# Layer 1's graph attention: projection of raw rows on centred weights, scores spread by DMA, and another order of mask loads

## The chip, the cores and the metric

The kernel runs on one core of a Trainium2 chip. The metric is the device time of one execution in microseconds (us). A core has five engines that run beside each other and meet in semaphores: TensorE (PE in the profile; PEld is its weight load), VectorE (DVE), ScalarE (ACT), GpSimd (POOL) and SyncE (SP, which here only issues DMAs). ACT, POOL and SP have each a queue for DMAs of their own; all of them share 16 DMA engines.

## What is computed

A network of two layers on 2708 rows of 256 numbers, each with a graph attention and a feed-forward part with experts. The change is in layer 1's graph attention:

```python
def _L1_gnn_ref(X, adj, W, b, S):        # X is the layernorm of x
    Xp = X @ W.T + b
    f = Xp.shape[1]
    n = X.shape[0]
    a_src = Xp @ S[:f]
    a_dst = Xp @ S[f:]
    e = jax.nn.leaky_relu(a_src[:, None] + a_dst[None, :])   # slope 0.01
    mask = (adj != 0) | jnp.eye(n, dtype=bool)
    e = jnp.where(mask, e, -jnp.inf)
    attn = jax.nn.softmax(e, axis=1)
    return jax.nn.sigmoid(attn @ Xp)
...
x = x + _L1_gnn_ref(_layernorm(x, axis=-1), adj, L1_gnn_W, L1_gnn_b, L1_gnn_S)
x = x + _L1_ffn_ref((_layernorm(x, axis=-1))[None], ...)[0]
```

With s = a_src of row i and d = a_dst of neighbour j, a weight before the division by its row's sum is exp(max(s + d, 0.01 (s + d))). A factor that depends on i alone falls out in that division, so exp(s) may be taken out, and what is left is max(exp(d), exp(0.01 d - 0.99 s)).

## The kernel before

Rows go in 22 tiles of 128 (P; the last has 20), columns in two halves (KC = 2). Stages follow one another: `first` (layer 0's attention parts), `experts_blocks` for layer 0, `second` (layer 1's graph attention and its routing), `experts_blocks` for layer 1. The change is in `second` (line 1416) and in the weight preparation of `first` (`weight_folds`, line 311).

**The order** inside `first` and `second` is not written by hand. Each step is given to a `Plan` (line 74) by `add(engine, length, run, needs, take, give, rank, lands)`: an estimated length, the steps it needs, the buffers it takes and gives back, a rank, and for a DMA the time to land. `issue` simulates the engines with these estimates, at each moment lets the engine with the lowest ranked startable step go on, and emits instructions in that order. Every engine then runs its own list strictly in order. Where the plan sees TensorE idle for over 1.0 us, it puts in matmuls of no use (`nobody`, line 1670), which cover 0.75 of the gap.

**`experts_blocks` for layer 0** leaves two blocks of expert 7 (`LATE`) for `second`, whose weights lie in the upper half of `arena`. Each expert block ends in a scatter that adds its rows in DRAM (`add_rows`, line 617, on GpSimd's queue).

**`second`.** `some_blocks` (line 524) does the two LATE blocks: rows fetched (534), transposed (539), three `up` steps (561), gate, two `down` steps (584), and the join by line 617. Beside them, five DMAs on SP bring X from DRAM (1519, 1527); those for tiles 10 and up wait for LATE's joins. `prepare(t)` makes a tile's features:

- `stats` (VectorE, 267, 269, 1458) and `power` (GpSimd, 1462) give mean and inverse deviation, `scale` (1466) the normalised rows xn,
- `turn` (1472) transposes xn on TensorE, `back` (ACT, 1476) copies it out of PSUM,
- `times`: line 1481 multiplies by the 258 columns of `wx[1]` (256 of W, then W times both halves of S, so that columns 256 and 257 are s and d); line 1484 multiplies `wsb`, which is column 256 repeated 128 times, by the tile, so that s of its 128 rows stands on every partition,
- `parts` (VectorE, 1488, 1489) keeps s and d in `sd`, and `dcol`, which is -0.99 d plus a constant `shift`; `features` (ACT) copies s into `sb` (1492), writes exp(d) into the last column of `hb` (1493) and the features times exp(d) into the others (1494).

PSUM's banks limit this: `mm` has two, and each is held from `times` to the end of `features`.

`aggregate` then goes through four groups of six tiles i (the last has four). For each of the 22 tiles j: `weigh` (ACT, 1560) makes E = exp(-0.99 s + dcol) for the group's 768 rows, `mask` (VectorE) turns the loaded masks to 0 and 1 (1569), sets the diagonal (1573) and makes PT = max(E, 1) times mask (1575), and TensorE adds PT times `hb` to the group's accumulators, six products of two records each (1582). E and PT have three buffers each. After a group, `mean`, a sigmoid, `join` and the routing follow beside the next group's products.

The masks lie in DRAM as rows (`mb`) and are turned by DMA transposes on SP, one for each tile i. Group 0's go to `arena` in two halves (1549): the first to its lower half, after the first three X loads; the second to its upper half, where LATE's weights lie, after LATE's joins. Those of groups 1 to 3 (1545) are issued six at a time into one of two places, when it is free.

**`weight_folds`** works out the extra columns early in `first`: it writes them to `wx[1]` (339) and spreads column 256 into `wsb` (341). `centre` (866) is there already for layer 0's weights: it sums the rows of a weight by a matmul with ones (872) and takes the column means off (876).

Of the kernel before, what the change touches and what calls it, by code (L numbers as in the profile page):

```python
# [20 lines left out]
P = 128  # L21
N = 2708
C = 256
# [126 lines left out]
def adj_ffn_kernel(ctx, tc, x, adj, vecs, bias_rows, tab, w_gnn0, w_gnn1, wqkv, wo,  # L150
# [155 lines left out]

    wsb = const.tile([P, KC, P], F32, name="wsb")
    shift = const.tile([P, 1], F32, name="shift")
    wnorm = const.tile([P, 1], F32, name="wnorm")

    def weight_folds(add, pool, tile_, needs, rank):

        fold = small.tile([P, 2, KC], F32, name="fold", bufs=1)
        for w, col in ((wg[0], V_C1), (wg[1], V_SS)):
            v = {}

            def turn(w=w, v=v):
                v["pt"] = tile_().rearrange("p (k i c) -> p k i c", k=KC, i=KC)
                for k in range(KC):
                    for i in range(KC):  # L320
                        nc.tensor.transpose(v["pt"][:, k, i, :], w[:, i, k * P:(k + 1) * P], ident)

            def back(v=v):
                v["wT"] = pool.tile([P, KC, C], F32, tag="rT", name="wT", bufs=1)
                nc.scalar.copy(v["wT"].rearrange("p k c -> p (k c)"), v["pt"].rearrange("p k i c -> p (k i c)"))

            def times(v=v, col=col):
                v["pc"] = tile_()[:, :2 * KC].rearrange("p (i a) -> p i a", i=KC)
                for i in range(KC):
                    for k in range(KC):  # L330
                        nc.tensor.matmul(v["pc"][:, i, :], v["wT"][:, k, i * P:(i + 1) * P],
                                         vec[:, col + k:col + k + KC + 1:KC], start=(k == 0), stop=(k == KC - 1))

            def norm(v=v):
                wc = small.tile([P, KC, 2], F32, name="wc", bufs=1)
                nc.scalar.activation(wc, v["pc"], AF.Square, accum_out=wnorm)

            def spread(v=v):
                nc.vector.tensor_copy(wx[1][:, :, C:], v["pc"])
                for k in range(KC):  # L340
                    nc.vector.tensor_copy(wsb[:, k, :], wx[1][:, k, C:C + 1].to_broadcast([P, P]))

            a = add("PE", 0.6, turn, needs, take=["mm"], rank=rank)
            a = add("ACT", 0.6, back, [a], take=["rT"], give=["mm"], rank=rank)
            a = add("PE", 1.0, times, [a], take=["mm"], give=["rT"], rank=rank)
            if col == V_C1:
                add("ACT", 0.4, norm, [a], give=["mm"], rank=rank)
            else:
                add("DVE", 0.7, spread, [a], give=["mm"], rank=rank)
        v = {}  # L350
# [14 lines left out]
        a = add("PE", 0.3, sum_up, [a], take=["mm"], rank=rank)  # L365
        add("DVE", 0.2, shifted, [a], give=["mm"], rank=rank)


# [419 lines left out]
    def first(X, XB, norms, tops, hd, mb, xs, acc, arena, load_weights):  # L788
# [11 lines left out]
        with ExitStack() as s:  # L800
# [431 lines left out]
            folded = add("DVE", 0.4, fold, [rest], rank=1.0)  # L1232
            weight_folds(add, af, mm_tile, [rest], 45.0)
            cleared = [add("SP", 2.5, lambda e=e: clear(xs[0], e), [loaded[10 + e]], rank=10.5 + e, lands=3.0)
# [181 lines left out]
    def second(X, XB, xs0, x1, x2, sd, mb, xs, arena, load_weights):  # L1416
# [5 lines left out]


        groups = [range(i, min(i + GI, NT)) for i in range(0, NT, GI)]
        F = C + 1
        with ExitStack() as s:
# [6 lines left out]
            sb = keep.tile([P, N], F32, name="sb")  # L1433
            dcol = keep.tile([P, NT], F32, name="dcol")


# [8 lines left out]
            add = plan.add  # L1445
            made, normed, got = [], [], []

            def prepare(t):
# [3 lines left out]

                bank = "po" if t < 8 else "mm"
                xt = X[:r, t, :]

                def stats():
                    v["mv"], v["pv"] = moments(xt, r), small.tile([P, 1], F32, tag="pv", name="pv")
                    nc.vector.tensor_scalar(v["pv"][:r], v["mv"][:r, 1:2], 1.0, 1e-5, ALU.mult, ALU.add)

                def power():  # L1460
                    v["rs"] = small.tile([P, 1], F32, tag="prs", name="prs")
                    nc.gpsimd.tensor_tensor(out=v["rs"][:r], in0=v["pv"][:r], in1=mhalf[:r, 0:1], op=ALU.pow)

                def scale():
                    v["xn"] = work.tile([P, C], F32, tag="xn", name="xn")
                    nc.vector.tensor_scalar(v["xn"][:r], xt, v["mv"][:r, 0:1], v["rs"][:r],
                                            ALU.subtract, ALU.mult)

                def turn():
                    v["pt"] = pt = (pso if bank == "po" else psm).tile([P, 4, P], F32, tag=bank, name="pt")  # L1470
                    for k in range(KC):
                        nc.tensor.transpose(pt[:, k, :r], v["xn"][:r, k * P:(k + 1) * P], ident[:r, :r])

# [4 lines left out]
                def times():  # L1478
                    v["pn"] = pn = psm.tile([P, 4 * P], F32, tag="mm", name="pn")
                    for k in range(KC):  # L1480
                        nc.tensor.matmul(pn[:r, :C + 2], v["xT"][:, k, :r], wx[1][:, k, :],
                                         start=(k == 0), stop=(k == KC - 1))
                    for k in range(KC):
                        nc.tensor.matmul(pn[:, 3 * P:3 * P + r], wsb[:, k, :], v["xT"][:, k, :r],
                                         start=(k == 0), stop=(k == KC - 1))

                def parts():
                    nc.vector.tensor_copy(sd[:r, t, :], v["pn"][:r, C:C + 2])
                    nc.vector.tensor_scalar(dcol[:r, t:t + 1], sd[:r, t, 1:2], SLOPE - 1.0, shift[:r], ALU.mult, ALU.add)

                def features():
                    nc.scalar.copy(sb[:, t * P:t * P + r], v["pn"][:, 3 * P:3 * P + r])
                    nc.scalar.activation(hb[:r, t, C:], v["pn"][:r, C + 1:C + 2], AF.Exp)
                    nc.scalar.activation(hb[:r, t, :C], v["pn"][:r, :C], AF.Copy, scale=hb[:r, t, C:])

                a = add("DVE", 0.85, stats, [loads[sum(t >= e for e in ends)]], take=["mv"], rank=rank)
                a = add("POOL", 0.6, power, [a], rank=rank)
                a = add("DVE", 0.42, scale, [a], take=["xn"], give=["mv"], rank=rank)
                a = add("PE", 0.3, turn, [a], take=[bank], give=["xn"], rank=rank)
                a = add("ACT", 0.4, back, [a], take=["xT"], give=[bank], rank=rank)  # L1500
                a = add("PE", 1.3, times, [a], take=["mm"], give=["xT"], rank=rank)
                b = add("DVE", 0.3, parts, [a], rank=rank)
                made.append(add("ACT", 0.9, features, [a, b], give=["mm"], rank=rank))

# [11 lines left out]

            loads, late, ends = [], [], (2, 7, LATE_T, NT - 1)
            for a, b in zip((0,) + ends, ends):
                loads.append(add("SP", 0.45 * (b - a), lambda a=a, b=b: nc.sync.dma_start(
                    out=X[:, a:b, :], in_=x1[a * P:b * P, :].rearrange("(t p) c -> p t c", p=P)),  # L1520
                    late, rank=-9.0, lands=12.5 if a == 0 else 11.0 if a < LATE_T else 7.0))
                if b == LATE_T:
# [7 lines left out]
            numbered = add("POOL", 0.3, lambda: nc.gpsimd.iota(  # L1530
                XR[:, :, C:C + 1].bitcast(I32), pattern=[[P, NT], [0, 1]], base=0, channel_multiplier=1), late, rank=-5.0)
            for t in range(NT):
                prepare(t)

            def aggregate(g, tiles):
# [4 lines left out]

                def masks():
                    v["mk"] = mks[int(side[g][-1])]
                    for i in tiles:
                        a = (i - tiles[0]) * P
                        nc.sync.dma_start_transpose(out=v["mk"][:, :, a:a + P], in_=mb[i * P:(i + 1) * P, :])

                def masks_by_tile(half):
                    for i in range(half * GI // 2, (half + 1) * GI // 2):
                        nc.sync.dma_start_transpose(out=by_tile[:, i, :, :], in_=mb[i * P:(i + 1) * P, :])

                if g == 0:
                    a = add("SP", 2.8 * GI // 2, lambda: masks_by_tile(0), loads[:3], take=[side[g]], rank=-8.0, lands=2.0)
                    got.append(add("SP", 2.8 * GI // 2, lambda: masks_by_tile(1), [a] + late, rank=-8.0, lands=2.0))
                else:
                    got.append(add("SP", 2.8 * len(tiles), masks, got[-1:], take=[side[g]], rank=rank, lands=2.0))

# [5 lines left out]
                def mask(j):  # L1562
# [11 lines left out]
                    v["PT", j] = p = work.tile([P, GI * P], F32, tag="PT", name="PT")  # L1574
                    nc.vector.scalar_tensor_tensor(wide(p), wide(v["E", j]), 1.0, m, ALU.max, ALU.mult)  # L1575

# [9 lines left out]
                for j in range(NT):  # L1586
                    a = add("ACT", 0.85, lambda j=j: weigh(j), [made[j]] + [made[i] for i in tiles], take=["E"],
                            rank=rank + j)
# [804 lines left out]
```

## Time and profile before

| | |
|---|---|
| median of 3 runs | 1506.64 us (1506.54 to 1509.68) |
| the profiled execution | 1506.29 us, of which its span 1504.5 |
| mean granted TensorE clock | 0.982 |
| TensorE busy in the span | 1417.7 us, 94% |
| VectorE, ACT, GpSimd busy | 762.5, 567.4, 529.9 us |
| line 1582, the products | 968 records, 228.5 us, first at 870.8, last at 1127.5 |
| line 1481, the 258 columns | 88 records, from 839.7 to 906.8 |
| line 1484, the scores on every partition | 88 records, from 840.7 to 907.4 |
| line 1560, the exponentials | 88, first at 855.0 |

A line of a group of instructions names the line of the kernel, the engine, the operation, what it writes and reads, and the shapes; then come the busy time, the mean of one in ns, and how long the engine stood idle just before them, with what ended the wait. In a line of the timeline the first two numbers are start and length in us. A line of busy time by stretch gives the engines' busy us in that stretch, then the granted clock (1.00 is full), the busy share of the DMA engines and what they moved.

### The profile page before, as it was taken

The page shows a single profiled execution, that of the slowest core. Times are in us where ns is not written, and L with a number is a line of the kernel's source. Part 1 is how long each engine was busy: PE and PEld are TensorE (multiplying, and loading weights), DVE is VectorE, ACT ScalarE, POOL GpSimd, SP SyncE. Part 2 cuts the span into 40 slices and gives each one's busy share as a digit, 9 for nine tenths or more (in the row PEclk, how much of TensorE's full clock was granted, in tenths as well). Part 3 has the DMA queues.
Part 4 walks back from the last instruction along what each step waited for, and adds up shares of the span by engine and source line. Part 5 has one row for each costly group of instructions (what it writes and reads, how often), then busy time and mean ns, then how long its engine had stood idle before and what let it go on. Part 6 is the DMA issues. An engine that isn't in the chain of part 4 may idle for free. (4 is left out here: it accounts for less than half of the span.)

```text
span 1504.5 us, 21112 instructions
## 1 busy us (share of the span) xinstructions
PE 1417.7 (94%) x7488; PEld 1030.2 (68%) x7488; DVE 762.5 (51%) x1647; ACT 567.4 (38%) x1134; POOL 529.9 (35%) x681
## 2 busy tenths in 40 slices
PE   5878989989999999999999989999999999999995
PEld 5633433433335888888888778888769878888884
DVE  5688999966676322222222564766745322222221
ACT  2576776755554322222221443444323212122220
POOL 5577668782152221222222310030434122222222
PEclk9999999999999999999999999999999999999998
DMA  7599757430011666656411860633412965566111
GB/s 261 190 298 291 256 193 235 146 121 8 7 41 42 172 194 176 182 150 185 113 15 22 183 133 1 137 80 98 154 48 75 273 190 140 160 173 169 15 18 20
DMA packets 198519, 201.83 MB, mean 134 GB/s; under 512 B 93248, under 2 KB 168520, under 8 KB 195696
## 3 DMA queue, kind: packets, MB, share of 16 engines
q1 hardware_dynamic: 173782, 170.96, 37.4%
q0 software_dynamic: 20352, 25.85, 9.7%
q10 hardware_dynamic: 4270, 3.58, 0.7%
q8 instruction: 61, 1.00, 0.3%
q14 instruction: 54, 0.44, 0.1%
HBM read 128.46 MB, written 56.37 MB: 123 GB/s over the span
## 5 line engine op out<-in xcount | busy, mean ns | idle before, releaser
L2065 PE MATMUL pup<-xTs,arena 128*128 128x256 f32 (+2 forms) x1320 | 252.8, 350 | 0.6 <-ACT xTs L2048 0.6
L2065 PEld LDWEIGHTS pup<-xTs,arena 128*128 128x128 f32 (+1 forms) x1320 | 219.5, 190 | 28.3 <-PE y L2130 2.3
L1582 PE MATMUL po<-hb,PT 128*128 128x257 f32 (+2 forms) x968 | 228.5, 390 | 4.0 <-DVE PT L1575 4.0
L2069 ACT ACTIVATE sl<-pup 128x256 f32<-128x256 f32 (+1 forms) x210 | 73.6, 350 | 370.8 <-PE pup L2065 369.1
L1582 PEld LDWEIGHTS po<-hb,PT 128*128 128x128 f32 (+2 forms) x968 | 177.3, 189 | 44.0 <-issue 13.1
L2070 DVE TENSOR_TENSOR hT<-sl,pup 128x256 f32<-128x256 f32 (+1 forms) x210 | 79.6, 379 | 229.0 <-ACT sl L2069 228.7
L1106 ACT ACTIVATE e<-stt 128x1024 f32<-128x1024 f32 (+1 forms) x132 | 125.4, 986 | 93.6 <-PE stt L1100 68.5
L617 POOL DMA_INDIRECT out<-ys,XR x45 | 69.4, 1542 | 246.7 <-DVE ys L2083 110.0
L1145 DVE TENSOR_TENSOR es<-es,e 128x1024 f32<-128x1024 f32 x104 | 138.0, 1327 | 29.8 <-ACT e L1106 23.1
L617 POOL DMA_INDIRECT acc<-ys,XR x45 | 69.8, 1552 | 226.3 <-DVE ys L2083 94.5
L1100 PE MATMUL stt<-qT,kT 64*128 64x512 f32 (+1 forms) x528 | 132.6, 612 | 6.3 <-ACT e L1106 6.1
L2080 PE MATMUL y<-arena,hT 128*128 128x256 f32 x612 | 136.7, 379 | 0.0
L1809 POOL DMA_INDIRECT xs<-XR,place x88 | 93.4, 1061 | 92.8 <-DVE mk L1569 41.3
L2080 PEld LDWEIGHTS y<-arena,hT 128*128 128x128 f32 x612 | 114.3, 190 | 14.5
L1126 PE MATMUL o<-e,V 128*64 128x512 f32 (+1 forms) x528 | 123.3, 590 | 0.0
L1560 ACT ACTIVATE E<-sb,dcol 128x768 f32<-128x768 f32 (+1 forms) x88 | 75.1, 859 | 108.5 <-DVE PT L1575 108.2
L2083 DVE TENSOR_SCALAR ys<-y,XR 128x256 f32<-128x256 f32 x71 | 34.3, 484 | 141.2 <-PE y L2080 141.1
L2065 PE MATMUL pup<-xTs,room 128*128 128x256 f32 (+3 forms) x528 | 99.9, 346 | 0.0
L1100 PEld LDWEIGHTS stt<-qT,kT 64*128 64x128 f32 x528 | 44.4, 187 | 78.1 <-issue 61.7
L2065 PEld LDWEIGHTS pup<-xTs,room 128*128 128x128 f32 (+1 forms) x528 | 85.4, 189 | 9.8 <-PE y L2130 0.8
L1126 PEld LDWEIGHTS o<-e,V 128*64 128x64 f32 x528 | 33.2, 137 | 69.9 <-issue 55.4
L974 DVE MAX8 tops<-arena 128x8 f32<-128x2708 f32 (+1 forms) x22 | 65.3, 2970 | 1.8 <-DMA arena<-in_adj 1.8
(316 smaller groups left out, 2026.0 us busy)
## 6 DMA issues: line engine op xcount, KB each, us to landing
more<-in_w SPq DMA_DIRECT2D x60, 640.0 KB
arena<-in_adj SPq DMA_DIRECT2D x21, 1354.0 KB
arena<-in_w SPq DMA_DIRECT2D x36, 640.0 KB
mb<-mb SPq DMA_DIRECT2D x44, 352.0 KB
XR<-xs SPq DMA_DIRECT2D x80, 134.0 KB
xs<-none SPq DMA_DIRECT2D x16, 536.0 KB
room<-in_w SPq DMA_DIRECT2D x12, 640.0 KB
acc<-X SPq DMA_DIRECT2D x21, 128.0 KB
```

The costliest lines, as they stand in the source:

```text
L617: nc.gpsimd.indirect_dma_start(out=acc[:, :], out_offset=bass.IndirectOffsetOnAxis(ap=tokens.bitcast(I32), axis=0), in_=ys, in_offset=None ...
L1100: nc.tensor.matmul(st[:r, g, c0(sb):], kT[a:b, sb * P:sb * P + r], qT[a:b, t0 + (sb == t0 + 1):t0 + 2, :, :], start=True, stop=True)
L1106: nc.scalar.activation(e[:r, :, c0(sb):], v[sb, "st"][:r, :, c0(sb):], AF.Exp, scale=1.0 / HD ** 0.5)
L1126: nc.tensor.matmul(v["o"][g * HD:(g + 1) * HD, c:], V[:r, sb, g * HD:(g + 1) * HD], v[sb][:r, g, c:], start=(n + i == 0), stop=(n + i == t ...
L1145: nc.vector.tensor_tensor(es, es, v[sb][:r, :, c:], ALU.add)
L1560: nc.scalar.activation(e[:q, :n], sb[:q, i0:i1], AF.Exp, bias=dcol[:q, j:j + 1], scale=SLOPE - 1.0)
L1582: nc.tensor.matmul(v["po", i][:r, :F], v["PT", j][:q, a:a + r], hb[:q, j, :], start=(j == 0), stop=(j == NT - 1))
L1809: i = nc.gpsimd.indirect_dma_start(out=xs[:, :], out_offset=bass.IndirectOffsetOnAxis(ap=at, axis=0), in_=src, in_offset=None)
L2065: nc.tensor.matmul(pp[:to, i, :B, :], wn[:, c, :], xT[:, c, :B, :], start=(c == 0), stop=(c == KC - 1))
L2069: nc.scalar.activation(sl[:, :B, :], pp[:, 0, :B, :], AF.Silu)
L2070: nc.vector.tensor_tensor(hT[:, n, :B, :], sl[:, :B, :], pp[:, 1, :B, :], ALU.mult)
L2080: nc.tensor.matmul(y, hT[:, n, b, :], w[3][:, n, :], start=(n == 0), stop=(n == NHC - 1))
```

## The change

- **Projection.** `centre` is called for `wx[1]` with its two extra columns, after `weight_folds`. `prepare` transposes the raw rows of X; the product is multiplied by the inverse deviation `rsx` when it is copied out. `stats` and `power` become steps of their own for pairs of tiles (`factors`), and are needed by `parts` only; `power` has two GpSimd instructions. The `scale` step, `wsb` and line 1484 are gone.
- **Scores.** `parts` writes s and d as before, scaled by `rsx`. When a group's tiles have theirs, ACT's queue stores the group's s to a row in DRAM, and then loads that row into `sb` on all 128 partitions. `weigh` needs that load.
- **Limit.** `hb` keeps the features without exp(d) and a column of ones; exp(d) goes into `ecol`, and line 1575 takes max(E, exp(d)). `dcol` has 0.01 d.
- **Masks and loads.** The first half of group 0's masks is issued ahead of the X loads, with no step to wait for but the use of its place; the second half waits for LATE's last `down`. Masks of the other groups are a step for each tile. X's loads are cut at other tiles, and the plan's estimates of loads and masks are other ones.

```diff
-                for k in range(KC):
-                    nc.vector.tensor_copy(wsb[:, k, :], wx[1][:, k, C:C + 1].to_broadcast([P, P]))
...
-            weight_folds(add, af, mm_tile, [rest], 45.0)
+            centre(wx[1], wx[1], C + 2, [weight_folds(add, af, mm_tile, [rest], 45.0)], 45.0)
...
+            ecol = keep.tile([P, NT], F32, name="ecol")
+            rsx = keep.tile([P, NT], F32, name="rsx1")
+            nc.gpsimd.memset(hb[:, :, C:], 1.0)
...
+            srow = dram.tile([1, NT * P], F32, name="srow")
+
+            def factors(tiles):
...
+                def power():
+                    r, k, t = rows(tiles[0]), len(tiles), tiles[0]
+                    pv = small.tile([P, 2], F32, tag="pv2", name="pv2")
+                    nc.gpsimd.tensor_scalar(pv[:r, :k], v["mv"][:r, :k, 1], 1.0, 1e-5, ALU.mult, ALU.add)
+                    nc.gpsimd.tensor_tensor(out=rsx[:r, t:t + k], in0=pv[:r, :k], in1=mhalf[:r, :k], op=ALU.pow)
...
-                bank = "po" if t < 8 else "mm"
+                bank = "po" if t < LATE_T else "mm"
...
-                        nc.tensor.transpose(pt[:, k, :r], v["xn"][:r, k * P:(k + 1) * P], ident[:r, :r])
+                        nc.tensor.transpose(pt[:, k, :r], xt[:, k * P:(k + 1) * P], ident[:r, :r])
...
-                    for k in range(KC):
-                        nc.tensor.matmul(pn[:, 3 * P:3 * P + r], wsb[:, k, :], v["xT"][:, k, :r],
-                                         start=(k == 0), stop=(k == KC - 1))
 
                 def parts():
-                    nc.vector.tensor_copy(sd[:r, t, :], v["pn"][:r, C:C + 2])
-                    nc.vector.tensor_scalar(dcol[:r, t:t + 1], sd[:r, t, 1:2], SLOPE - 1.0, shift[:r], ALU.mult, ALU.add)
+                    nc.vector.tensor_scalar(sd[:r, t, :], v["pn"][:r, C:C + 2], rsx[:r, t:t + 1], None, ALU.mult)
+                    nc.vector.tensor_scalar(dcol[:r, t:t + 1], sd[:r, t, 1:2], SLOPE, shift[:r], ALU.mult, ALU.add)
 
                 def features():
-                    nc.scalar.copy(sb[:, t * P:t * P + r], v["pn"][:, 3 * P:3 * P + r])
-                    nc.scalar.activation(hb[:r, t, C:], v["pn"][:r, C + 1:C + 2], AF.Exp)
-                    nc.scalar.activation(hb[:r, t, :C], v["pn"][:r, :C], AF.Copy, scale=hb[:r, t, C:])
+                    nc.scalar.activation(hb[:r, t, :C], v["pn"][:r, :C], AF.Copy, scale=rsx[:r, t:t + 1])
+
+                def factor():
+                    nc.scalar.activation(ecol[:r, t:t + 1], sd[:r, t, 1:2], AF.Exp)
...
+                b = add("DVE", 0.45, parts, [a, c], rank=rank)
+                parted.append(b)
+                a = add("ACT", 0.5, features, [b], give=["mm"], rank=rank)
+                made.append(add("ACT", 0.2, factor, [a], rank=rank))
...
-            loads, late, ends = [], [], (2, 7, LATE_T, NT - 1)
+            loads, late, ends = [], [], (2, 6, LATE_T, 16, NT - 1)
...
-                    late, rank=-9.0, lands=12.5 if a == 0 else 11.0 if a < LATE_T else 7.0))
+                    late, rank=-9.0, lands=4.0))
...
-                    a = add("SP", 2.8 * GI // 2, lambda: masks_by_tile(0), loads[:3], take=[side[g]], rank=-8.0, lands=2.0)
-                    got.append(add("SP", 2.8 * GI // 2, lambda: masks_by_tile(1), [a] + late, rank=-8.0, lands=2.0))
+                    half = GI // 2
+                    a = add("SP", 3.2 * half, lambda: masks_by_tile(0, half), [], take=[side[g]], rank=-10.0, lands=2.0)
+                    through = [e["needs"][0]["needs"][0] for e in late]
+                    got.append(add("SP", 3.2 * half, lambda: masks_by_tile(half, GI), [a] + through, rank=-9.5, lands=2.0))
                 else:
-                    got.append(add("SP", 2.8 * len(tiles), masks, got[-1:], take=[side[g]], rank=rank, lands=2.0))
+                    a = got[-1]
+                    for i in tiles:
+                        a = add("SP", 3.2, lambda i=i: masks(i), [a], take=[side[g]] * (i == tiles[0]), rank=rank, lands=2.0)
+                    got.append(a)
+
+                def spread_out():
+                    nc.scalar.dma_start(out=srow[0, i0:tiles[-1] * P + P].rearrange("(t p) -> p t", p=P),
+                                      in_=sd[:, tiles[0]:tiles[-1] + 1, 0])
+
+                def spread_in():
+                    nc.scalar.dma_start(out=sb[:, i0:i1], in_=srow[:, i0:i1].to_broadcast([P, n]))
+
+                a = add("ACT", 0.5, spread_out, [parted[i] for i in tiles], rank=-7.0 + g, lands=3.0)
+                row_in = add("ACT", 0.5, spread_in, [a], rank=-7.0 + g, lands=3.0)
...
-                    nc.vector.scalar_tensor_tensor(wide(p), wide(v["E", j]), 1.0, m, ALU.max, ALU.mult)
+                    nc.vector.scalar_tensor_tensor(wide(p), wide(v["E", j]), ecol[:q, j:j + 1], m, ALU.max, ALU.mult)
...
-                    a = add("ACT", 0.85, lambda j=j: weigh(j), [made[j]] + [made[i] for i in tiles], take=["E"],
+                    a = add("ACT", 0.85, lambda j=j: weigh(j), [made[j], row_in], take=["E"],
```

## Prediction

> **What bounds the kernel now.** I read the page's costliest groups first, then the busy time by stretch, then the order of time around the one stretch where TensorE is not full. Layer 1's products, line 1582, are its second largest group:
>
> ```profile
> L1582 PE MATMUL po<-hb,PT 128*128 128x257 f32 (+2 forms) x968 | 228.5, 390 | 4.0 <-DVE PT L1575 4.0
> ```
>
> They run from 870.8 to 1127.7 us, and TensorE idles only 4.0 us before them, once. The stretches before and after the first product (busy us of TensorE, its weight loads, VectorE, ScalarE, GpSimd; granted clock; DMA share; GB/s):
>
> ```profile
> 853.00:860.00 7.00, 5.22 (x29) 4.02 (x27) 2.24 (x11) 6.08 (x18) 0.54 (x1) 1.00 1.13 251
> ...
> 865.00:870.00 5.00, 1.58 (x8) 1.28 (x8) 0.83 (x3) 0.18 (x1) 0.21 (x1) 0.93 1.07 229
> 870.00:876.00 6.00, 5.23 (x12) 4.20 (x13) 5.55 (x17) 2.57 (x5) 1.08 (x2) 0.50 1.05 228
> ...
> 890.00:940.00 50.00, 50.00 (x252) 44.08 (x251) 23.59 (x51) 22.18 (x48) 0.06 (x1) 1.00 0.00 1
> ```
>
> From 890 on TensorE is full and nothing else is; before, there is a hole at 867 to 870.8 and then a clock of 0.50 until 876. So in this stage two things are worth time: the moment of the first product, and every matmul taken away behind it. What ends the hole, on TensorE and VectorE, and what SP issues, in order of time (start, length):
>
> ```profile
> 866.22 0.60 PE L1484 MATMUL pn<-xTs,wsb 128*128 128x128 f32 x4
> ...
> 869.03 0.36 DVE L1569 TENSOR_SCALAR arena<-arena 128x768 bf16<-128x768 bf16 x1 [4.22 <-DMA arena<-mb]
> ...
> 869.76 0.96 DVE L1575 SCALAR_TENSOR_TENSOR PT<-E,arena 128x768 f32<-128x768 f32 x1
> ...
> 870.77 5.94 PE L1582 MATMUL po<-hb,PT 128*128 128x257 f32 x14 [3.95 <-DVE PT L1575]
> ```
>
> ```profile
> 830.48 1.86 SPq L1519 DMA_DIRECT2D X<-acc  x3
> 832.38 12.32 SPq L1549 DMA_TRANSPOSE arena<-mb  x3
> 851.29 0.38 SPq L1519 DMA_DIRECT2D X<-acc  x1
> 851.77 0.52 SPq L1527 DMA_DIRECT2D X<-acc  x1
> 852.39 13.81 SPq L1549 DMA_TRANSPOSE arena<-mb  x3
> 866.25 19.45 SPq L1545 DMA_TRANSPOSE mk<-mb  x6
> ```
>
> VectorE waits 4.22 us for the second half of group 0's masks, issued 852.39 to 866.2 and landed at 868.9, after the last LATE join (line 617, 847.45) and two X loads. The first exponential ran at 855.0, so its own inputs were ready 14 us earlier. **The masks, not the preparation, set the first product.**
>
> **What the Trainium skill says.** (1) "DMA: Bandwidth & Descriptors", section "Rules for kernel authors": a run that is not contiguous is lowered to one descriptor per element, and a DMA that reads what another wrote must wait for its completion. The trace of before has no 4-byte store, so neither is shown. (2) The same page, "Queues, rings and completion order": a DMA engine takes turns between queues packet by packet. The trace agrees in kind: line 617's scatters land in 3.7 to 5.8 us, the longest being the one issued beside the mask transposes. (3) "TensorE: Matmul & The Clock Gate", part 1: an idle window of about 3.4 us halves the clock. Agrees: 3.95 us idle, then 0.50.
>
> **The change, part by part.** The sum is made against the profiled execution, 1506.29 us (span 1504.5); the median of the runs is 0.35 higher.
>
> *Matmuls removed.* Per tile, line 1484's four records go. Their worth is the spacing in the full stretch:
>
> ```profile
> 882.21 1.04 PE L1481 MATMUL pn<-wg,xTs 128*128 128x258 f32 x4
> 883.09 0.61 PE L1484 MATMUL pn<-xTs,wsb 128*128 128x128 f32 x4
> 883.53 1.90 PE L1582 MATMUL po<-hb,PT 128*128 128x257 f32 x8
> ```
>
> 0.88 us for line 1481, 0.44 for 1484, and 0.22 for the two transposes (881.12 to 881.34). A tile's preparation on TensorE falls from 1.54 to 1.10 us.
>
> *First half of the masks moved* ahead of the X loads on SP. It needs only the arena's lower half, which expert 6's last line-2080 matmuls leave at 809.2, so it runs about 809 to 819 (three at 3.3 us, as line 1545 shows) and lands by 822. It meets line 617's scatters at 817.5: up to 2.1 us (5.8 less 3.7) on one of them, so X loads start at 830.5 to 832.6. The plan puts tile 0's transpose into the gap at 838.6, after LATE's second `up`; X landed 2.8 us after issue before, so this is covered, by 3 us. *Second half*: released by LATE's last `down` (846.6 before; I take 845, as the gap is filled sooner) instead of the join; 3 x 3.3 us, then 2.2 to land: 857. Behind it on SP wait the three X loads for tiles 10 to 21, from 851.3 to about 855; they land about 862 and are used behind the first product. The group-1 masks follow, as before, to some 876; they are used from 930.
>
> *Scores by DMA.* Tiles 0 and 1 fit in TensorE's gap 838.6 to 843; from 845 a tile every 1.2 us or so (two PSUM banks, each held for line 1481, `parts` and `features`) gives tile 5's `parts` at 849.6. Then ACT issues a store of 768 elements of 4 bytes, 48 per DMA engine, and waits for it before the broadcast load of 128 rows of 3072 bytes. Bounds for one small packet, from the page:
>
> ```profile
> q1 hardware_dynamic: 173782, 170.96, 37.4%
> ...
> q10 hardware_dynamic: 4270, 3.58, 0.7%
> ```
>
> Share x 16 x 1504.5 / packets is 52 ns and 39 ns. Alone: 48 x 40 ns = 1.9 us; taking turns with the transposes: 48 x 92 = 4.4. With about 2 us to complete (an estimate; the same page, section "Anatomy of one DMA", gives 2.0; the 256 KB X load took 2.8 in all) the store is 3.9 or 6.4 us, the load 3.5 with its data. A gain is excluded: before, this cost nothing. During group 0's turn the transposes run, so 6.4: store issued 849.9, done 856.3, load done 860.3. Exponential 0.93, line 1575 0.96: **first product 862.2**, not 870.8. Masks (857) no longer decide.
>
> *ACT waits.* The load waits in ACT's queue; the plan allows 3.2 us for the store. Queued behind it are `back`, `features` and `weigh`, and TensorE in its fixed order waits for those. Group 0's wait falls where TensorE idles anyway. Group 1's (tile 11, about 870, still beside transposes): 6.4 - 3.2 = 3.2, less some 0.2 of slack, as prepared tiles go ahead of products: 3.0. Group 2's, without transposes: 3.9 - 3.2 - 0.2 = 0.5. Group 3's: no preparation is left, and three PT buffers of 2.6 us each cover it: 0; uncovered, 0.7.
>
> *Other engines.* ACT loses line 1492 (0.27), keeps an exponential; VectorE loses the `scale` pass (0.41) and line 1458; line 1575 gets its limit from a column, same 768 elements, 0.96 assumed (a pointer scalar in line 1466 costs nothing extra: 256 elements, 0.41). VectorE was busy 23.6 of 50, so even 0.2 more is hidden. `power` becomes two GpSimd operations per pair, about what two were; it is needed only at `parts`, and stands behind LATE's joins as before. The memset of `hb` is of the size of line 300's, 0.31, while GpSimd waited 3.5.
>
> *Layer 0's stage.* `centre` adds four records like line 872's (0.9 us) and two VectorE passes (2 x 0.42) at 65 us, less two copies of 0.23. VectorE paces there: +0.4; from 0 to 1.3.
>
> *Sum.* First product 8.6 earlier. Behind it, before: 10 tiles x 1.54 = 15.4; after: 12 x 1.10 = 13.2, as tiles 10 and up load later: 2.2. The hole before it (tile 9 is done by about 854, fillers cover half of 8 us) is long enough that I keep the slow clock: it costs 2.6 (5.2 us at half rate) in both. 8.6 + 2.2 - 3.0 - 0.5 - 0.4 = 6.9. Everything behind, to the end of the kernel, is TensorE's (100% in most stretches) and moves with it: 1506.3 - 6.9 = **1499.4 us**.
>
> **Rivals.** *The small stores are dear (slower).* With w the time of one 4-byte packet, the first product is at 857.8 + 48w, and groups 1 and 2 each stall TensorE by 48w - 1.4; the gain is 17.6 - 3 x 48w: zero at 48w = 5.9, w = 122 ns. For: nothing in the trace is that small, and the skill's same page, "Specifications", has stores under 512 bytes read before they are written. Against: the mean packet takes 39 to 52 ns. At 200 ns: 48w = 9.6, 11.2 us slower, 1517.5. *The scores are hidden.* The store completes as planned, ACT never stalls, masks decide (first product 858.6), the fillers keep the clock: 12.2 + 2.2 + 2.6 - 0.4 = 16.6, 1489.7. For: ACT has spare time, and the plan fills gaps. Against: DMA is full then (1.07 to 1.13). *The masks don't move.* If SP held the first half until LATE's `down`, X loads would be behind it, at 857 instead of 830.5; preparation of six tiles (8), landing (3) and scores (12) put the first product at 880: some 7 slower, 1513. Against: before, the first half was issued at 832.4, while LATE still read the upper half.
>
> **How the numbers follow.** Forecast 0.55 (gains of 3 to 12.5, its own range 1494 to 1503); scores hidden 0.15 (1490 to 1494); small stores at 101 to 143 ns 0.10 (within 3 us, which is 0.2%, about what a measurement can tell from no change); above that 0.15; masks unmoved 0.05. Faster 0.70, same 0.10, slower 0.20. The range runs from 1490 to the upper end of "same", 1509.5, and leaves out the slower cases.
>
> **What would show it.** Line 1549's first three issues near 809 and its second before 847; the first product at 862, with VectorE or ACT waiting for the row load and not for `arena<-mb`; no line-1484 records; ACT idle before the second row load of some 3 us, with TensorE idle beside it. The prediction is wrong if the store takes over 8 us, if another wait holds the first product past 866, or if the two plans' new order opens holes elsewhere in TensorE's time.

## The result, and the profile after

The changed kernel takes 1522.19 us (median of 4 runs, 1522.00 to 1523.85) beside 1508.16 us of the kernel before (4 runs, 1506.54 to 1512.35). The ratio on record is 1.0104, with a 95% interval of 1.0078 to 1.0129 (the two medians alone divide to 1.0093): slower by 1%, where 1499.4 was predicted. The profiled execution took 1522.13 us, of which its span 1520.4, at a mean granted clock of 0.972.

The products are now line 1616. In the costliest groups, their idle time has gone from 4.0 to 16.6 us:

```profile
L1616 PE MATMUL po<-hb,PT 128*128 128x257 f32 (+2 forms) x968 | 231.6, 393 | 16.6 <-DVE PT L1609 13.6
```

Busy time by stretch (columns as before: TensorE, its weight loads, VectorE, ScalarE, GpSimd; granted clock; DMA share; GB/s):

```profile
857.00:864.00 7.00, 0.00 (x0) 0.00 (x0) 0.00 (x0) 0.14 (x2) 0.00 (x0) 0.53 1.02 213
864.00:872.00 8.00, 5.83 (x17) 4.69 (x18) 6.44 (x17) 5.55 (x7) 1.15 (x4) 0.56 1.12 236
...
881.00:892.00 11.00, 3.50 (x11) 2.84 (x11) 2.94 (x10) 2.10 (x6) 1.47 (x4) 0.69 1.19 108
...
904.00:909.00 5.00, 0.17 (x1) 0.00 (x0) 0.00 (x0) 0.40 (x2) 0.00 (x0) 0.97 0.00 0
909.00:916.00 7.00, 6.87 (x18) 3.78 (x19) 1.66 (x4) 2.69 (x9) 0.00 (x0) 0.54 0.21 56
```

There was one hole, a stretch in which TensorE idles, before the first product; there are now three. Behind each the clock is 0.5 for some us (the 0.69 of 881 to 892 is a mean over the stall and what follows it). In the third, from 904.2 to 908.2, no engine works and no DMA moves anything. What ends them, in order of time, on ACT and then on TensorE:

```profile
846.06 0.39 ACTq L1582 DMA_DIRECT2D srow<-sd  x1
...
855.73 0.34 ACTq L1586 DMA_DIRECT2D sb<-srow  x1
856.12 0.47 ACT L1503 ACTIVATE hb<-pn,rsx 128x256 f32<-128x256 f32 x1 [7.09 <-DMA srow<-sd]
...
864.13 3.41 ACT L1594 ACTIVATE E<-sb,dcol 128x768 f32<-128x768 f32 x4 [6.99 <-DMA sb<-srow]
...
888.01 0.47 ACT L1503 ACTIVATE hb<-pn,rsx 128x256 f32<-128x256 f32 x1 [9.16 <-DMA srow<-sd]
...
898.81 0.37 ACTq L1582 DMA_DIRECT2D srow<-sd  x1
...
908.22 0.33 ACTq L1586 DMA_DIRECT2D sb<-srow  x1
908.60 0.47 ACT L1503 ACTIVATE hb<-pn,rsx 128x256 f32<-128x256 f32 x1 [6.48 <-DMA srow<-sd]
...
916.02 0.37 ACTq L1582 DMA_DIRECT2D srow<-sd  x1
...
924.18 0.33 ACTq L1586 DMA_DIRECT2D sb<-srow  x1
```

```profile
866.17 3.79 PE L1616 MATMUL po<-hb,PT 128*128 128x257 f32 x8 [12.48 <-DVE PT L1609]
...
888.54 0.69 PE L1486 MATMUL pt<-ident,X 128*128 128x128 f32 x2 [7.50 <-ACT hb L1503]
...
909.13 0.69 PE L1486 MATMUL pt<-ident,X 128*128 128x128 f32 x2 [4.96 <-ACT hb L1503]
```

The wait is written at line 1503, `features`, but that step only stands behind the load of the row (1586), which waits for the store (1582). From the store's issue to the load's issue it takes 9.7 us for group 0, 12.8 for group 1 (874.81 to 887.63) and 9.4 for group 2; group 3's store has 512 elements in place of 768 and takes 8.2. The masks did move. On SP, and VectorE's first use of them:

```profile
787.03 23.00 SPq L1566 DMA_TRANSPOSE arena<-mb  x3
...
833.98 10.55 SPq L1566 DMA_TRANSPOSE arena<-mb  x3
...
849.40 38.58 SPq L1562 DMA_TRANSPOSE mk<-mb  x6
```

```profile
850.62 0.36 DVE L1603 TENSOR_SCALAR arena<-arena 128x768 bf16<-128x768 bf16 x1
...
865.10 1.02 DVE L1609 SCALAR_TENSOR_TENSOR PT<-E,ecol,arena 128x768 f32<-128x768 f32 x1 [13.86 <-ACT E L1594]
```

VectorE turns masks at 850.6 and then waits 13.86 us for an exponential.

**A common starting point.** The LATE blocks' first transpose starts at 825.0 us before, at 821.2 after, and between 820.6 and 828.6 in the profiles listed below, which differ from the changed kernel only behind it or by small stages far ahead of it. So I read each profile from that point to the first product and to the first `mean` of group 0 (the group's end), in us. These two columns and the ratio of measured times are:

| kernel | first product | group 0's end | ratio to before (95%) |
|---|---|---|---|
| before | 45.7 | 120.0 | |
| changed | 44.9 | 134.3 | 1.0104 (1.0078 to 1.0129) |
| a1, the same again | 45.9 | 135.3 | 1.0087 (1.0059 to 1.0114) |
| e1, plan knows the waits | 52.2 | 117.6 | 0.9981 (0.9967 to 0.9996) |
| e2, store in runs of 512 B | 39.6 | 111.7 | 0.9951 (0.9938 to 0.9963) |
| e3, store twice | 49.5 | 142.5 | 1.0147 (1.0118 to 1.0175) |
| e4, masks' part alone | 36.8 | 113.7 | 0.9970 (0.9958 to 0.9983) |
| e5, scores on TensorE | 34.4 | 108.7 | 0.9922 (0.9898 to 0.9946) |
| e7, row load on POOL | 45.5 | 117.3 | 1.0000 (0.9980 to 1.0020) |
| e9, e2 and the plan | 42.3 | 111.8 | 0.9925 (0.9900 to 0.9949) |

### The profile page after: what moved, and what is told of

Read it like the earlier page. It is cut to its first block, busy times and chain, and to the rows that moved or that the text cites. A ratio compares the mean times of both kernels' runs of the same rounds, so it can differ in the third digit from the quotient of the medians.

```text
span 1520.4 us, 20941 instructions
## 1 busy us (share of the span) xinstructions
PE 1419.2 (93%) x7430; PEld 1027.1 (68%) x7430; DVE 759.6 (50%) x1603; ACT 563.8 (37%) x1112; POOL 530.4 (35%) x684
## 5 line engine op out<-in xcount | busy, mean ns | idle before, releaser
L1616 PE MATMUL po<-hb,PT 128*128 128x257 f32 (+2 forms) x968 | 231.6, 393 | 16.6 <-DVE PT L1609 13.6
L2117 DVE TENSOR_SCALAR ys<-y,XR 128x256 f32<-128x256 f32 x71 | 34.4, 484 | 141.8 <-PE y L2114 141.7
L1609 DVE SCALAR_TENSOR_TENSOR PT<-E,ecol,arena 128x768 f32<-128x768 f32 (+1 forms) x44 | 44.8, 1018 | 55.6 <-PE po L1616 36.6
```

The costliest lines, as they stand in the source:

```text
L1616: nc.tensor.matmul(v["po", i][:r, :F], v["PT", j][:q, a:a + r], hb[:q, j, :], start=(j == 0), stop=(j == NT - 1))
```

## The experiments

**Theory:** the store of a few hundred 4-byte elements lands late, and ACT, whose queue holds the wait, starves TensorE. **Rivals:** the stores and the transposing loads slow each other whatever the order; or the new order of steps itself opens the holes.

### e1: the plan knows how long the DMAs take

```diff
-spread_out, [parted[i] for i in tiles], rank=-7.0 + g, lands=3.0)
+spread_out, [parted[i] for i in tiles], rank=-7.0 + g, lands=9.5)
-spread_in, [a], rank=-7.0 + g, lands=3.0)
+spread_in, [a], rank=-7.0 + g, lands=8.5)
```

> The changed kernel with one thing altered: the plan that orders each engine's instructions is told that the store of a group's scores lands after 9.5 us and the load of the row after 8.5 us (3.0 and 3.0 in the changed kernel), so that it puts other ACT work between a store, its load and the first exp that uses the row. The instructions are the same. Theory A, ACT stands still for a store that takes longer than the plan knew, and TensorE starves behind it (stalls of 7.5 and 5.0 us in groups 0 and 1 and some 5 us of lowered clock after them): about 1505 to 1511 us, no gap of ACT over 2 us on the row store inside group 0. Rival B, the stores and the transposing loads of masks compete and slow each other whatever the order is: within 3 us of the changed kernel's 1522.

Measured: 0.9981, group 0's end 16.7 us sooner than in the changed kernel. What ACT waited for from 840 to 930 us, in the changed kernel and in this one (total, times, longest):

```profile
ACT hb L1503 <- DMA srow<-sd: 22.7, 3, 9.2
```

```profile
ACT hb L1503 <- DMA srow<-sd: 2.7, 1, 2.7
```

The store is no faster (849.50 to 859.97 for group 0), and the time comes back. The first product is 7.3 us later than in the changed kernel, but TensorE does projection meanwhile, save for a hole of 6.49 us in which it waits for rows of X. This is what the theory said, but a gap of ACT of 2.7 us was left where I expected none over 2.

### e7: the wait in another queue

```diff
-nc.scalar.dma_start(out=sb[:, i0:i1], in_=srow[:, i0:i1].to_broadcast([P, n]))
+nc.gpsimd.dma_start(out=sb[:, i0:i1], in_=srow[:, i0:i1].to_broadcast([P, n]))
...
-row_in = add("ACT", 0.5, spread_in, ...)
+row_in = add("POOL", 1.0, spread_in, ...)
```

> The changed kernel with the load of the row issued by POOL in place of ACT: the store is as slow as before, but the wait for it stands in POOL's queue, where nothing is behind it that the projection needs. Theory A, the loss is ACT standing still behind the wait: ACT's gaps on the store (23 us together) are gone, TensorE keeps on preparing tiles in them, first product no earlier than 862, time 1502 to 1510 (0.996 to 1.002 of the kernel before). Rival B, the products wait for the row itself, whoever issues it: 1516 to 1524.

Measured: 1.0000, group 0's end 17.0 us sooner than in the changed kernel. POOL now stands in the wait:

```profile
861.48 0.65 POOL L1586 DMA_DIRECT2D sb<-srow  x1 [9.02 <-DMA srow<-sd]
894.79 0.65 POOL L1586 DMA_DIRECT2D sb<-srow  x1 [9.20 <-DMA srow<-sd]
...
```

and TensorE has one hole, of 12.64 us before the first product. Two ways of taking ACT out of the wait, one by order and one by queue, give back the same 17 us. What they share is that ACT's queue no longer stands in the wait, so it is that and not the order of the steps by itself that costs them. (In e7 the plan puts the steps in order anew too.)

### e2: the same bytes in runs of 512

```diff
+def flat(): nc.tensor.transpose(v["pr"][:len(tiles), :P], sd[:, tiles[0]:tiles[-1] + 1, 0], ident)
+def flat_back(): nc.scalar.copy(v["sr"][:len(tiles)], v["pr"][:len(tiles), :P])
...
-nc.scalar.dma_start(out=srow[...].rearrange("(t p) -> p t", p=P), in_=sd[:, tiles[0]:tiles[-1] + 1, 0])
+nc.scalar.dma_start(out=srow[...].rearrange("(t p) -> t p", p=P), in_=v["sr"][:len(tiles)])
```

> The changed kernel with the group's scores turned on TensorE first (one transpose of a 128 x 6 column block per group and one ACT copy, together some 0.5 us), so that the store writes 6 runs of 512 bytes in place of 768 elements of 4 bytes. Theory A1, the store is dear because it is made of 768 small elements: store to landing falls from 8 to 12 us to some 3 us, ACT's gaps on it fall to 0 to 2 us, first product some 5 us earlier, time about 1503 to 1510. Rival A2, the store is dear because of a fixed latency, or because the transposing loads stand in its queues: it still takes 7 us or more, time 1518 to 1524.

Measured: 0.9951, below the range of theory A1; group 0's end 22.6 us sooner than in the changed kernel. ACT's issues of group 0's store and load:

```profile
846.95 0.26 ACTq L1590 DMA_DIRECT2D srow<-sr  x1
849.41 0.35 ACTq L1594 DMA_DIRECT2D sb<-srow  x1
```

2.5 us (2.2 to 3.2 in the other groups), beside the same masks and X loads. So the traffic alone does not make a store slow, and with the store repaired the rest of the change gains: 8.3 us to group 0's end. What is left is the load of the row, 8.7 us beside that traffic, with a hole of 5.86 us before the first product.

### e3: every store twice

```diff
+for row in (srow2, srow):
     nc.scalar.dma_start(out=row[...].rearrange("(t p) -> p t", p=P), in_=sd[:, tiles[0]:tiles[-1] + 1, 0])
```

> The changed kernel with every store of a group's scores issued twice, first to a row that nobody reads. Theory A1, a price per small element (48 to each of 16 DMA engines at about 0.15 us): each store to its landing takes about 7 us more, so about 5 to 7 us on the first product and on each of the two stalls of ACT, time some 1537 to 1545. Rival A2, a fixed latency with cheap elements: about 1 us more at each place, time 1523 to 1527.

Measured: 1.0147. Group 2's store, without other traffic, takes 11.6 us from the first issue to the load's (911.29 to 922.91) where one took 9.4; group 0's 11.8 for 9.7. 768 more elements cost 2.2 us, of which 0.6 is the second issue: neither the 7 us of theory A1 nor the 1 us of A2, and the time lies between their ranges too, but both nearer to A2. A price per packet is not the cause.

### Where the store's time is

Group 2's store in the changed kernel, issued at 898.81 and waited for until 908.2, in stretches of 1 us (the last two numbers are the DMA engines' share and GB/s):

```profile
899.00:900.00 1.00, 1.00 (x7) 0.87 (x6) 0.29 (x2) 0.78 (x3) 0.00 (x0) 1.00 0.21 2
900.00:901.00 1.00, 1.00 (x8) 0.84 (x7) 0.87 (x1) 0.28 (x2) 0.00 (x0) 1.00 0.16 1
901.00:902.00 1.00, 1.00 (x6) 0.89 (x5) 0.15 (x1) 0.97 (x2) 0.00 (x0) 1.00 0.00 0
...
907.00:908.00 1.00, 0.00 (x0) 0.00 (x0) 0.00 (x0) 0.00 (x0) 0.00 (x0) 1.00 0.00 0
```

The packets are over by 901; 7 us of the wait come after the last of them. I call this part, from the last packet to the release of what waits, the landing. The packets themselves take 0.37 us of 16 engines for some 770 of them, which is 8 ns each. The Trainium skill, "DMA: Bandwidth & Descriptors", section "Anatomy of one DMA", says that most of a DMA's fixed time is the wait for the confirmation that the last byte is in the target memory, HBM being the slowest target. That section is about DMAs that GpSimd issues, and this store goes out on ACT's queue. The trace agrees on the place; the size, 7 us and not its 2.0, is what the next two runs look into. Both are e2's kernel, executed once each, with stores on SP beside its work, each with a small load that waits for it.

### e6: six kinds of small stores

```diff
+def probe(k, dst, src, first):
+    nc.sync.dma_start(out=dst, in_=src)
+    nc.sync.dma_start(out=back[:, k * 8:k * 8 + n], in_=first)
```

> The kernel with the store in runs of 512 bytes, and beside its work six probes on SP's queue in two quiet stretches, each a store from the scores' tile and a small load of what it wrote, so that the time from the store's issue to the load's issue is issue to landing. In order: (0) 768 elements of 4 bytes as the changed kernel stores them, (1) 128 such elements, (2) 768 elements, each on a 64-byte line of its own, (3) 768 elements with each partition's six next to each other in HBM, (4) 768 pairs of 8 bytes, (5) 768 elements to SBUF in place of HBM. Theory L, several writes of a few bytes to the same line of HBM wait for each other: (0) and (1) take 8 to 9 us, (2) and (5) 2 to 4, (4) clearly less than (0). Theory N, a price per small write to HBM whatever its line: (1) 2.5 to 3.5, (2) and (4) as (0), 8 to 9.5, (5) 2 to 4. Theory F, it is the sending side (48 elements to an engine): (5) as (0), (1) 3 to 4.

```profile
874.39 0.54 SPq L1457 DMA_DIRECT2D probe<-sd  x1
885.48 0.24 SPq L1458 DMA_DIRECT2D back<-probe  x1
885.78 0.34 SPq L1457 DMA_DIRECT2D probe<-sd  x1
894.33 0.23 SPq L1458 DMA_DIRECT2D back<-probe  x1
894.62 0.36 SPq L1457 DMA_DIRECT2D probe<-sd  x1
898.60 0.23 SPq L1458 DMA_DIRECT2D back<-probe  x1
...
956.00 0.64 SPq L1457 DMA_DIRECT2D probe<-sd  x1
964.32 0.24 SPq L1458 DMA_DIRECT2D back<-probe  x1
964.60 0.39 SPq L1457 DMA_DIRECT2D probe<-sd  x1
968.92 0.24 SPq L1458 DMA_DIRECT2D back<-probe  x1
969.20 0.66 SPq L1457 DMA_DIRECT2D flat<-sd  x1
971.39 0.73 SPq L1458 DMA_DIRECT2D back<-flat  x1
```

The first stretch was not quiet throughout. ACT issued the load of group 2's row into the second store, and most of its bytes moved at 896 to 898, beside the third:

```profile
887.55 0.35 ACTq L1614 DMA_DIRECT2D sb<-srow  x1
```

From a store's line to the next: 11.1 us for 768 packed elements (some mask traffic to 880 beside them), 8.6 for 128 packed ones (beside the row's load), 4.0 for 768 spread 64 bytes apart (beside it too), 8.3 for 768 with each partition's six adjacent (masks beside them to 958), 4.3 for 768 pairs, 2.2 for 768 to SBUF. The same number takes half the time or less when the elements lie apart, as theory L said, and the traffic beside the 4.0 made other stores longer, not shorter. N and F fall, by the third and the sixth. That a sixth of the elements takes nearly the same time isn't shown, as these 128 had the row's load beside them. What is shown without traffic is group 3's store in the changed kernel: two thirds of the elements, 8.2 us for 9.4.

### e10: the spacing alone

```diff
+strided = [dram.tile([P, w], F32, name=f"probe{w}") for w in (1, 2, 4, 8, 16, 32)]
+nc.sync.dma_start(out=strided[k][:, 0:1], in_=sd[:, 0:1, 0])
+nc.sync.dma_start(out=back[:, k * 8:k * 8 + 1], in_=strided[k][0:1, 0:1])
```

> The kernel with the store in runs of 512 bytes, and beside its work six probes on SP's queue in two quiet stretches: always 128 elements of 4 bytes, one from each partition, stored to HBM at a stride of 4, 8, 16, 32, 64 and 128 bytes, so that 16, 8, 4, 2, 1 and 1 of them fall on a 64-byte line, each store followed by a load of 4 bytes that waits for it. Theory L, writes to the same line wait for each other, some 0.4 us each: about 8.5, 5, 3.5, 2.7, 2.3 and 2.3 us from the store's issue to the load's. Rival G, the penalty belongs to writes packed without gaps (a stream that is gathered and flushed late), not to their number on a line: 8.5 at 4 bytes, and one equal value from 8 bytes on.

```profile
879.36 0.54 SPq L1455 DMA_DIRECT2D probe<-sd  x1
888.62 0.24 SPq L1456 DMA_DIRECT2D back<-probe  x1
888.92 0.34 SPq L1455 DMA_DIRECT2D probe<-sd  x1
894.58 0.23 SPq L1456 DMA_DIRECT2D back<-probe  x1
894.87 0.34 SPq L1455 DMA_DIRECT2D probe<-sd  x1
896.53 0.23 SPq L1456 DMA_DIRECT2D back<-probe  x1
...
969.04 0.33 SPq L1455 DMA_DIRECT2D probe<-sd  x1
970.44 0.24 SPq L1456 DMA_DIRECT2D back<-probe  x1
```

and on ACT's queue, the load of group 1's row:

```profile
881.21 0.34 ACTq L1608 DMA_DIRECT2D sb<-srow  x1
```

Measured, for 128 elements of 4 bytes 4, 8, 16, 32, 64 and 128 bytes apart: 9.3, 5.7, 1.7, 3.2, 1.4 and 1.4 us. But the three slowest are also the three that had other traffic beside them: the first the last masks and the row's load, the second the rest of that load (most of its bytes moved at 890 to 893) and group 2's store, the fourth mask loads and stores of X. The changed kernel's packed stores took 0.3 and 3.4 us more beside traffic (9.7 and 12.8) than without it (9.4), which is less than the 7.9 between 4 and 64 bytes here. So e6 and the ends of this row agree that close elements land late, as L and G both say; how the time falls between 4 and 32 bytes isn't shown. L's fixed 0.4 us for each write on a line asks for 3.5 us at 16 bytes, where 1.7 was measured. G asks for one value from 8 bytes on, and the undisturbed three (1.7, 1.4, 1.4) are near that; the 5.7 at 8 bytes would refute it only if it did not come from the traffic. What in the memory makes close writes wait, and the size of the stretch they share, stay open.

The Trainium skill's page "DMA: Bandwidth & Descriptors", section "Specifications", says that stores under 512 bytes are read before they are written. Stores of 4 bytes at 1.4 us show that a small size alone is not dear here; if that reading is the mechanism, it costs only when neighbours are close.

### e4: the masks' part alone

```diff
-a = add("SP", 2.8 * GI // 2, lambda: masks_by_tile(0), loads[:3], take=[side[g]], rank=-8.0, lands=2.0)
-got.append(add("SP", 2.8 * GI // 2, lambda: masks_by_tile(1), [a] + late, rank=-8.0, lands=2.0))
+a = add("SP", 3.2 * GI // 2, lambda: masks_by_tile(0), [], take=[side[g]], rank=-10.0, lands=2.0)
+through = [e["needs"][0]["needs"][0] for e in late]
+got.append(add("SP", 3.2 * GI // 2, lambda: masks_by_tile(1), [a] + through, rank=-9.5, lands=2.0))
```

(and the changed kernel's cuts and estimates of the X loads, in the kernel before).

> The kernel before with one part of the change alone: the order of the loads for group 0 (first half of the masks ahead of the X loads, second half from the fifth block's products on, X loads cut at 2, 6, 13, 16 and 22, told to land after 4 us). Scores stay on TensorE, columns centred by the folds of before. Theory M, the masks set the first product in the kernel before: first product at about 857 to 862 us in place of 870.8, time 1496 to 1501. Rival N, TensorE or ACT takes the place of the masks at once, or the rest of the prep is in the way of the products: first product not before 866, time 1502 to 1507.

Measured: 0.9970, first product at 862.7 us, 8.9 earlier from the common start; group 0's end 6.3 earlier, as part of what came before the first product now comes behind it (9 tiles are projected before it, where 12 were). The first product is where theory M had it, within 0.7 us; the time, taken as a ratio to the 1508 of before, is in rival N's range. So the masks did set the first product, and most but not all of that is worth time.

### e5: the scores on TensorE, no DMA

```diff
+nc.vector.tensor_scalar(dg[:r, :r], ident[:r, :r], sd[:r, t, 0:1], None, ALU.mult)
+nc.tensor.matmul(v["pn"][:, 3 * P:3 * P + r], allones[:r], v["dg"][:r, :r], start=True, stop=True)
+nc.scalar.copy(sb[:, t * P:t * P + r], v["pn"][:, 3 * P:3 * P + r])
```

(`spread_out` and `spread_in` are left out.)

> The changed kernel with the scores spread on TensorE and no DMA: per tile DVE scales the identity by the tile's score column, one 128 x 128 product with ones puts the scores on all partitions, and ACT copies them into the row (about 0.22 us of TensorE, 0.35 us of ACT and 0.2 us of DVE a tile more than in the changed kernel). Theory A, all that the change loses it loses at the DMA: no gap of ACT on a row, no PE stall above 2 us after the first product, first product at 850 to 858 us, time 0.4 to 1.2% below the kernel before. Rival B, masks or the shorter prep leave TensorE idle anyway before the first product: no better than the store in runs of 512 bytes (0.995 of the kernel before), and a gap of TensorE of 4 us or more named on the masks or on ACT.

Measured: 0.9922, the fastest of all by its middle value. First product at 856.1, with this before it:

```profile
856.07 2.87 PE L1614 MATMUL po<-hb,PT 128*128 128x257 f32 x12 [0.62 <-DVE PT L1607]
```

No hole of over 1 us and no slow clock between 840 and 932; group 0 ends 3.0 us sooner than in e2. So 22 products more on TensorE cost less than a row's way through HBM by the profile, while the intervals of the two ratios overlap. Theory A.

### e9 and a1: what was left

e9 is e2 with `lands=9.0` for the load of the row.

> The kernel with the store in runs of 512 bytes, with the plan told that the load of the row lands after 9.0 us in place of 3.0 (8.7 us were measured for the first group's, beside masks and layer inputs). The instructions are the same. Theory A, the 5.9 us in which TensorE stands ahead of the first product can be filled with tiles of the projection: no gap of TensorE above 2 us there, 2 to 6 us below the kernel with the runs, 0.990 to 0.993 of the kernel before. Rival B, the tiles put there wait for layer inputs that land late: no gain, 0.994 to 0.997.

Measured: 0.9925, but group 0's end is at 111.8 us where e2 has 111.7, and the intervals overlap. TensorE's hole became 3.38 us elsewhere, and the first product came 2.7 us later. The ratio is the one that theory A named and the profile that of rival B: I count it as no gain shown.

> The changed kernel once more, with a second profile and its ratio on this chip. In its first profile group 2 took 68.2 us from the first mean of the group before to its own, where the kernel before took 62.0 and the kernels with other stores 62.0 to 64.4: some 5 us of starving at 1018 to 1030 us. Theory P, that belongs to the change (its later loads of masks and rows of that time meet the scatters): group 2 takes 67 us or more again. Rival O, it was of that one execution: 62 to 65 us. In both, the stalls of 7.5 and 5.0 us behind ACT in group 0 and 1 are there again, within 1 us, and the ratio is 1.008 to 1.013.

Measured: 1.0087; stalls of 8.17 and 5.53 us behind ACT; group 2 took 63.6 us. Rival O: the 68.2 us of the first profile do not belong to the change. e10's profile, with another store, has such a group again (67.6).

## Why the prediction was wrong

I go by its steps, in us from the common start where a moment is meant.

- **What bounds the kernel: right.** With the masks alone moved (e4) the first product came 8.9 us earlier. That a us of the first product is a us of the end was too simple: 6.3 of 8.9 reached group 0's end.
- **Matmuls removed: right in size.** Line 1495 keeps its 0.87 to 0.88 us a tile, line 1484's records are gone, and 12 tiles lie behind the first product, as forecast. e2 ends group 0 2.0 us ahead of e4, for the 2.2 forecast, but the two differ in their holes too, so how near this comes is in part luck. Line 1609 takes 1.02 us where 0.96 was assumed, which VectorE hides. The 0.4 forecast for layer 0's stage is lost in the spread of the starts.
- **Masks: right, and earlier than said.** The first half was issued from 787.0, not 809. The second was issued from 834.0, not 845, which is 12.8 and 20 from the common start: only the last of its three loads (841.6) came behind LATE's last `down` (838.8 to 841.6), which the prediction and the account of the change have as the release of all three. VectorE had masks in use at 850.6.
- **The store: this step failed.** "48 x 40 ns = 1.9 us", with "about 2 us to complete", gave 3.9 alone and 6.4 beside the transposes. Measured 9.4 and 9.7 to 12.8. Both terms were wrong, and the second by more: a packet of 4 bytes takes some 8 ns in the records, less than the queue's mean, and its landing 7 us, not 2. I had taken both bounds from mean packet durations, and the landing from the page's 2.0 and a load of 256 KB in rows of 1 KB. None of these has close small writes to HBM in it.
- **The load: mis-sized.** 4.0 with its issue; 8.4 in group 0 (855.73 to 864.13), beside X loads and masks. e2's is 8.7 with no such store, so the traffic is enough to explain it. After group 2, in a quiet stretch, the DMA was busy only to 912, 3.8 after its issue at 908.2.
- **The first product:** 37.2 forecast, 44.9 measured. The store was issued when I said (24.8, forecast 24.9); 9.7 - 6.4 = 3.3 of the store and 8.4 - 4.0 = 4.4 of the load are the whole of the 7.7.
- **ACT waits: mechanism right, sizes off.** 3.0 and 0.5 of TensorE's time were forecast; 7.50 and 4.96 came, 9.0 more.
- **The slow clock: left out.** I kept 2.6 us in both kernels. Each stall brought its own half clock (0.56, 0.69 and 0.54 in the stretches above): 14.4 us of work behind them at half rate (866.2 to 871, 888.5 to 891.7, 909.1 to 915.5), that is 7.2 lost, 4.6 more.
- **Sum.** 7.7 + 9.0 + 4.6 = 21.3 of the 21.6 us by which group 0 ended later (134.3) than the steps said (120.0 - 7.3 = 112.7). With the 4-byte store replaced (e2) it ended at 111.7.
- **The rivals.** "The small stores are dear" had the sign, and that its 1517.5 was near is luck. Its mechanism, a time w of each packet, is not what happened: twice the packets cost 2.2 us and not 48w. "Masks don't move" is refuted by SP's lines above. The prediction named a store of over 8 us as what would undo it, and that is there; the first product, at 866.2, was held by this store and the row's load and not by another wait.

In the first profile, a start 3.8 us earlier and some 6 us of a late group 2 (68.2, before 62.0) lie on top. The start is within the spread of the profiles listed, which share the code ahead of it, and the late group is not there in a1.

## What to carry to other kernels

A column that was stored to HBM element by element cost its landing here, not its packets: turn it on TensorE first and store rows, or spread it by a product with ones and leave HBM out. A wait for a DMA stands in the queue of the engine that issues what waits: put it on an engine with nothing behind it, or tell the scheduler the real time; either gave back 17 of 22 us here. And a stall of TensorE is to be priced with the half clock after it, which every hole of 3.4 us or more brought in this stage of the profiles above (the shortest is e9's 3.38).

## What the runs showed of the hardware

- The landing of a store of small elements depends on how close they lie in HBM: 768 elements of 4 bytes took 8.3 to 9.4 us packed (e6's fourth store, nearly without other traffic, and group 2's in the changed kernel, without any), and 4.0 us 64 bytes apart, beside other traffic (e6). Two thirds of the packed elements still took 8.2.
- Other transfers are slow while such a store is under way. From 850 to 855, with the same X loads and masks issued just before, the changed kernel still waits for group 0's store, and in e2 the store in runs has landed. The last number of each line is what the DMA engines moved, in GB/s, first in the changed kernel, then in e2:

```profile
850.00:855.00 5.00, 3.69 (x33) 3.50 (x31) 1.01 (x4) 0.00 (x0) 0.00 (x0) 1.00 0.68 45
```

```profile
850.00:855.00 5.00, 4.31 (x39) 4.12 (x37) 1.01 (x4) 0.56 (x2) 0.00 (x0) 1.00 1.18 265
```

  The issue of the first of group 1's masks took 15.1 us in the changed kernel and 8.1 in e2, that of all six 38.6 and 24.0. The row's load that e6 issued beside 128 packed elements agrees: most of its bytes moved 8.5 to 10 us after its issue, where in e2 those of the same load (issued at 886.83) moved within 3.2. So half of the rival "the stores and the transposing loads slow each other" holds, the store slows the loads. It is not where the time went: in e1 they move as slowly beside the store (53 GB/s from 850 to 860), and its time is that of the kernel before or less. How the store holds the others up isn't shown.
